# Three cross-attention tiles ahead of the loop instead of two

## The chip, the cores and the metric

The kernel runs on one NeuronCore of a Trainium2 chip. The metric is the device time of one launch in microseconds (us). Three runs of the kernel before took 3867.34, 3873.22 and 3873.66 us, so its median is 3873.22 us.

## The reference

One decoder layer is computed in float32 on x of shape 4 x 512 x 512 (2048 tokens, 512 channels), in three residual steps:

```python
x = x + attn(layernorm(x))           # gated delta rule, 16 heads, state 128 x 128 per head
x = x + xattn(layernorm(x), ctx)     # cross attention on 256 context rows, fake-quantised
x = x + ffn(layernorm(x))            # causal self attention with rope, then 2 of 8 experts
```

The cross attention of a token needs only that token's row after the first step: q = h Wq + bq, quantised per head; for each of 16 heads of width 32 the softmax over 256 keys, quantised to 255 levels; the weighted values; and a projection with Wp. The third step begins with a layer norm and an RMS norm of the result; keys, values and queries follow from that.

## The kernel before

All work is cut into 16 tiles of 128 tokens (NT = 16; a sequence is four tiles). There are three stages.

The first stage is the delta rule. It walks over 32 pairs of heads (NP = 32: four sequences by eight pairs). For pair m it runs `stage3(m)`, the recurrence over four chunks of 128 tokens, and beside it the output projection of pair m-1 (`output(m-1)`) and the preparation of later pairs. In the last two rounds the preparation has run out, so that little is left beside the recurrence. `output` of a sequence's last pair also scales the rows and writes them to DRAM (`x1d`), from which the cross attention reads its tiles (`xi`).

The second stage, the loop, is put together by `weave`. It holds four streams: `attention(i)` of tile i, `qkv(i)` 1.36 tiles ahead of it, the cross attention (`crossing(i)`, which carries `norms(i-1)` in its first steps) some tiles ahead, and what follows the attention (`rest_of`, `route`). Each stream is a chain of Python generators; `weave` gives every generator a start and a length in tiles and always takes the next step of the one that is furthest behind. The order written in this way is then arranged again by the compiler's scheduler, engine by engine[...].

The third stage runs the experts. It is not touched.

The pieces that the change concerns:

- `cross(i)` (lines 225 to 323) is one tile's cross attention. In order: layer norm (L131 to L137), transposes (L200), the query projection (L242), bias and quantisation (L244 to L217, on VectorE, ScalarE and GpSimd in turn), transposes (L200), four rounds of scores (L262), exponentials (L269), rounding (L274 on GpSimd, L278 on VectorE) and transposes (L287), the weighted values (L300), the output projection (L318), and bias and residual (L320, L321). It writes the result to DRAM (`x2d`, L322) and keeps it in SBUF as `x2`, a tile with two buffers.
- `xi` is loaded at the start of a cross attention (L232), or ahead by the one before it (L308), which before the change happens from tile 2 on.
- `norms(i)` (L1000 to L1018) reads `x2`, normalises twice and gives `hTs[i]`, which `qkv(i)` needs. `x3`, its tile in between, has one buffer and is stored to DRAM (`x3d`, L1006).
- In the last round of the first stage, `cross(0)` runs beside `stage3(31)` and `output(30)`, two steps of it for each step of the others. After that round `output(31)` and `cross(1)` run beside each other (L951). Then come the weights' first loads (`load_q`, `load_o`), `norms(0)` and the loop, whose cross attention begins with tile 2.
- `X` and `W` (L1325) are the lead and the spacing of the cross attention in the loop, in tiles.

`turns` takes its generators one after the other, each by its number of steps; `chain` runs them one behind the other. Loads and stores named `nc.sync` are issued by SyncE (SP in the profile), in order.

Of the kernel before, what the change touches and what calls it, by code (L numbers as in the profile page):

```python
# [40 lines left out]
NT = B * S // P  # L41
# [57 lines left out]
def decoder(ctx: ExitStack, tc: tile.TileContext, a: dict, out: bass.AP):  # L99
# [39 lines left out]
    def chain(*gs):  # L139
        for g in gs:  # L140
            yield from g
# [31 lines left out]
    def run(*gs):  # L173
        for g in gs:
            for _ in g:
                pass
# [50 lines left out]
    def cross(i):  # L227

        xi = xis.pop(i, None)
        if xi is None:  # L230
            xi = wx.tile([P, D], F32, name="xi", bufs=2)
            nc.sync.dma_start(xi, x1d[i])  # L232
            yield
            yield
        xn = wx.tile([P, D], F32, name="xn", bufs=1)
        yield from layernorm(xn.unsqueeze(1), xi.unsqueeze(1), wx)
        yield
        xT = transposed(xn, wx, "xT")
        yield
        pq = p_b.tile([P, D], F32, name="pb")  # L240
        for kd in range(KD):
            nc.tensor.matmul(pq, xT[:, kd, :], wq[:, kd, :], start=kd == 0, stop=kd == KD - 1)  # L242
        q = wx.tile([P, D], F32, name="xn", bufs=1)
        nc.vector.tensor_tensor(q, pq, bq, ALU.add)  # L244
        yield
        nc.scalar.mul(q, q, float(1.0 / np.sqrt(np.float32(HD2))))
        quantised(q, q, H2, HD2, wx)
        yield
        yield
        yield  # L250
        qT = transposed(q, wx, "x_qT", bufs=1)
        yield
        aT = wx.tile([P, KD, P], F32, name="xT")

        def scores(g0, r0, out):


            ps = [p_b.tile([P, 2, M], F32, name="pb") for _ in range(2)]
            for g in range(2):
                for r in range(2):  # L260
                    rs = slice((r0 + r) * HD2, (r0 + r + 1) * HD2)
                    nc.tensor.matmul(ps[r][:, g, :], qT[rs, g0 + g, :], x_kT[rs, g0 + g, :], start=True, stop=True)  # L262
            nm, ssum = (wx.tile([P, 4], F32, name=n) for n in ("nm", "ssum"))
            e = wx.tile([P, 4, M], F32, name="x_e")
            for r in range(2):
                nc.vector.tensor_reduce(nm[:, 2 * r : 2 * r + 2], ps[r], AX.X, ALU.max, negate=True)  # L266
                for g in range(2):
                    n = 2 * r + g
                    nc.scalar.activation(e[:, n, :], ps[r][:, g, :], AF.Exp, bias=nm[:, n : n + 1], accum_out=ssum[:, n : n + 1])  # L269
            yield  # L270


            ef = e.rearrange("p n m -> p (n m)")
            nc.gpsimd.tensor_scalar(ef, ef, 255.0, MAGIC, ALU.mult, ALU.add)  # L274
            nc.vector.tensor_scalar(ssum, ssum, 255.0, None, ALU.mult)
            nc.vector.reciprocal(ssum, ssum)
            yield
            nc.vector.scalar_tensor_tensor(e, e, MAGIC, along(ssum, M), ALU.subtract, ALU.mult)  # L278
            out.append(e)

        def turned(e, out):

            for r in range(2):
                tp = p_b.tile([P, 2, 2, P], F32, name="pb")
                for g in range(2):
                    for kt in range(2):
                        nc.tensor.transpose(tp[:, g, kt, :], e[:, 2 * r + g, kt * P : (kt + 1) * P], ident)  # L287
                eT = wx.tile([P, 2, 2, P], F32, name="x_eT", bufs=4)
                nc.scalar.copy(eT, tp)
                out.append(eT)  # L290
                yield

        def weighted(g0, eTs):

            pa = p_b.tile([P, 2, P], F32, name="pb")
            for g in range(2):
                for kt in range(2):
                    for r in range(4):
                        h = 4 * (g0 + g) + r
                        nc.tensor.matmul(pa[r * HD2 : (r + 1) * HD2, g, :], x_val[:, kt, h * HD2 : (h + 1) * HD2], eTs[r][:, g, kt, :], start=kt == 0, stop=kt == 1)  # L300
            nc.vector.tensor_copy(aT[:, g0 : g0 + 2, :], pa)
            yield

        es, eTs = [], []
        for u in range(5):
            if u == 3 and 1 < i < NT - 1:
                xis[i + 1] = wx.tile([P, D], F32, name="xi", bufs=2)
                nc.sync.dma_start(xis[i + 1], x1d[i + 1])  # L308
            if u < 4:
                yield from scores(u // 2 * 2, u % 2 * 2, es)  # L310
            if u > 0:
                yield from turned(es.pop(0), eTs)
            if u in (2, 4):
                yield from weighted(u - 2, eTs)
                eTs.clear()
        pw = p_b.tile([P, D], F32, name="pb")
        for kd in range(KD):
            nc.tensor.matmul(pw, aT[:, kd, :], wpj[:, kd, :], start=kd == 0, stop=kd == KD - 1)  # L318
        x2 = wx.tile([P, D], F32, name="x2", bufs=2)
        nc.vector.tensor_tensor(x2, pw, bp, ALU.add)  # L320
        nc.gpsimd.tensor_tensor(x2, x2, xi, ALU.add)  # L321
        nc.sync.dma_start(x2d[i], x2)  # L322
        x2s[i] = x2


    with ExitStack() as st:
# [593 lines left out]
        for m in range(NP):  # L920
            rest = []
            if m == NP - 2:
                first.close()
                x_keep = top.enter_context(tc.tile_pool(name="x_keep", bufs=1, side="right", reuse_waits="tile"))
                wq, wpj = (x_keep.tile([P, KD, D], F32, name=n) for n in ("wq", "wpj"))
                nc.sync.dma_start(wq, a["b_wq"].rearrange("(k p) c -> p k c", p=P))
                nc.sync.dma_start(wpj, a["b_wp"].rearrange("(k p) c -> p k c", p=P))
                bq, bp = rows(x_keep, "bq", "b_bq", D), rows(x_keep, "bp", "b_bp", D)
                x_kT, x_val = x_keep.tile([P, KD, M], F32, name="x_kT"), x_keep.tile([P, 2, D], F32, name="x_val")
                nc.sync.dma_start(x_kT, x_kT_d)  # L930
                nc.sync.dma_start(x_val, x_val_d)
            if m == NP - 1:
                second.close()
                wx = top.enter_context(tc.tile_pool(name="b_x", bufs=2, side="right", reuse_waits="tile"))
                rest.append((cross(0), 2))
            if m:
                rest.append((output(m - 1), 1))
            if m + 2 < NP:
                if (m + 2) % NHG == 0:
                    assert (m + 2) // NHG in seqs  # L940
                rest.append((stage1(m + 2), 2))
            if m + 1 < NP:
                rest.append((stage2_values(m + 1), 1))
                rest.append((stage2_inverse(m + 1), 2))
            if (m + 4) % NHG == 0 and (m + 4) // NHG < B:
                rest.append((prologue((m + 4) // NHG), 1))
            rest = turns(*rest)
            for _ in stage3(m):
                next(rest, None)
            run(rest)  # L950
        run(turns((output(NP - 1), 1), (cross(1), 2)))  # L951

# [7 lines left out]
    with ExitStack() as st:  # L962
# [37 lines left out]
        def norms(i):  # L1000


            x2 = x2s.pop(i)
            x3 = wq_.tile([P, D], F32, name="x3", bufs=1)
            yield from layernorm(x3.unsqueeze(1), x2.unsqueeze(1), small)
            nc.sync.dma_start(x3d[i], x3)  # L1006
            h = wq_.tile([P, D], F32, name="h3", bufs=1)
            ss = small.tile([P, 1], F32, name="rms_s")
            nc.scalar.activation(h, x3, AF.Square, accum_out=ss)
            yield  # L1010
            r = small.tile([P, 1], F32, name="rms_r")
            rsqrt(r, ss, small, add=1e-6, mul=1.0 / D)
            yield
            nc.vector.scalar_tensor_tensor(h, x3, r, ln1, ALU.mult, ALU.mult)
            yield
            hTs[i] = transposed(h, wq_, "hT", bufs=2)
            yield
# [276 lines left out]
        def crossing(i):  # L1294

            g = cross(i)
            return chain(turns((norms(i - 1), 1), (itertools.islice(g, 6), 1)), g)
# [24 lines left out]

        Q, X, W = 1.36, 3.1, 1.03  # L1325
        at_x = [(2 - X + (i - 2) * W, W, crossing(i), "cross") for i in range(2, NT)]
        at_x[-1] = (*at_x[-1][:2], last(chain(at_x[-1][2], norms(NT - 1))), "cross")
        at_q = [(i - Q, 1.0, qkv(i), "qkv") for i in range(NT)]
        at_q[-1] = (*at_q[-1][:2], last(at_q[-1][2]), "qkv")
# [2 lines left out]
        for i in range(NT - 1):  # L1332
# [3 lines left out]
            elif i == NT - 2:  # L1336
                g, kind = chain(g, route(12, 3)), "route"
            at_r.append((i + 1.06, 0.5, g, kind))
        run(norms(0))
        weave(at_a, at_q, at_x, at_r, [(NT - Q, 0.9, load_experts(), "load")])  # L1340
        w_gu, w_d = experts_w
        run(rest_of(NT - 1), route(NT - 1, 1))
# [182 lines left out]
```

## Time and profile before

| | before |
|---|---|
| median of three runs | 3873.22 us |
| the profiled execution, its own time | 3875.28 us |
| its span | 3873.5 us |
| PE busy | 3479.9 us (90%) |
| VectorE / ScalarE / GpSimd busy | 58% / 39% / 35% |
| last recurrence begins (first L704) | 2114.07 us |
| last matmul of cross(0) begins its group (L318) | 2164.06 us |
| last group of cross(1) (L318) | 2217.53 us |
| first projection of the loop (L1067) | 2221.49 us |
| last write of a cross attention result (L322) | 3425.4 us |
| first matmul of the last value product group (L1163), last start | 3565.8 us |

Times inside the execution count from the start of its span. A line such as L242 is a line of the kernel before. The profile of one matmul in float32 shows two instructions, so that eight L242 instructions are four matmuls. The timeline's columns are start, length, engine, line, operation, what is written and read, the number of merged instructions, and in brackets the idle time before them and what ended it.

### The profile page before, as it was taken

The page shows a single profiled execution, that of the slowest core. Times are in us where ns is not written, and L with a number is a line of the kernel's source. Part 1 is how long each engine was busy: PE and PEld are TensorE (multiplying, and loading weights), DVE is VectorE, ACT ScalarE, POOL GpSimd, SP SyncE. Part 2 cuts the span into 40 slices and gives each one's busy share as a digit, 9 for nine tenths or more (in the row PEclk, how much of TensorE's full clock was granted, in tenths as well). Part 3 has the DMA queues.
Part 4 walks back from the last instruction along what each step waited for, and adds up shares of the span by engine and source line. Part 5 has one row for each costly group of instructions (what it writes and reads, how often), then busy time and mean ns, then how long its engine had stood idle before and what let it go on. Part 6 is the DMA issues. An engine that isn't in the chain of part 4 may idle for free. (4 is left out here: it accounts for less than half of the span.)

```text
span 3873.5 us, 48929 instructions
## 1 busy us (share of the span) xinstructions
PE 3479.9 (90%) x16466; PEld 1984.5 (51%) x16466; DVE 2238.7 (58%) x5115; ACT 1523.7 (39%) x4190; POOL 1374.0 (35%) x1941
## 2 busy tenths in 40 slices
PE   5898989898989898989889879999999999898897
PEld 3455555555555555555545445555555555554443
DVE  5576657765766676657665546655665565554111
ACT  3334443334443434343433334444444444344121
POOL 1543554355335543554355222213212221211442
PEclk8899999998999999999999889999999999999898
DMA  5324332433234324333433245445544444456444
GB/s 163 109 71 126 104 103 78 130 104 114 78 106 129 104 77 120 105 102 100 120 88 111 72 154 161 139 147 158 163 132 140 145 139 141 137 174 206 82 82 92
DMA packets 391881, 465.56 MB, mean 120 GB/s; under 512 B 128451, under 2 KB 242115, under 8 KB 391440
## 3 DMA queue, kind: packets, MB, share of 16 engines
q1 hardware_dynamic: 380080, 438.03, 37.8%
q0 software_dynamic: 10112, 21.58, 3.1%
q8 instruction: 132, 2.16, 0.2%
q10 hardware_dynamic: 1440, 2.84, 0.2%
q14 instruction: 117, 0.96, 0.1%
HBM read 401.76 MB, written 64.81 MB: 120 GB/s over the span
## 5 line engine op out<-in xcount | busy, mean ns | idle before, releaser
L503 PE MATMUL pb<-xnT,w 128*128 128x512 f32 x2048 | 953.0, 604 | 0.0
L503 PEld LDWEIGHTS pb<-xnT,w 128*128 128x128 f32 x2048 | 381.0, 195 | 421.9 <-issue 417.8
L514 DVE SCALAR_TENSOR_TENSOR cv<-pb,pp,cv 128x511 f32<-128x511 f32 (+2 forms) x576 | 427.6, 742 | 153.0 <-ACT cv L511 144.0
L1067 PE MATMUL pb<-c_q,hT 128*128 128x512 f32 x768 | 360.7, 608 | 7.4 <-DMA c_q<-in_c_wq_dram 3.4
L644 POOL TENSOR_TENSOR iW<-iA,iT 32x31 f32<-32x31 f32 (+15 forms) x496 | 249.4, 503 | 212.3 <-DMA iA<-at_d 142.2
L825 PE MATMUL pb<-wot,og 128*128 128x512 f32 x512 | 265.9, 644 | 31.8 <-DVE og L796 26.5
L645 POOL TENSOR_TENSOR iT<-iT,iW 32x31 f32<-32x31 f32 (+15 forms) x496 | 275.2, 555 | 38.9
L511 ACT ACTIVATE cv<-pb,pp 128x512 f32<-128x512 f32 x192 | 148.2, 772 | 259.9 <-PE pb L503 259.4
L1173 PE MATMUL pw<-c_o,oT 128*128 128x512 f32 x512 | 241.8, 603 | 2.9 <-DVE oT L1165 2.9
L1067 PEld LDWEIGHTS pb<-c_q,hT 128*128 128x128 f32 x768 | 143.5, 195 | 165.4 <-issue 152.3
L1139 ACT ACTIVATE e<-pb,nm,rq 128x128 f32<-128x128 f32 (+3 forms) x256 | 157.0, 618 | 142.4 <-DVE nm L1137 108.8
L274 POOL TENSOR_SCALAR x_e<-x_e 128x1024 f32<-128x1024 f32 x64 | 68.7, 1074 | 329.4 <-ACT x_e L269 240.4
L644 DVE TENSOR_TENSOR iW<-iA,iT 32x31 f32<-32x31 f32 (+15 forms) x496 | 177.9, 359 | 12.4 <-DMA iA<-at_d 0.9
L645 DVE TENSOR_TENSOR iT<-iT,iW 32x31 f32<-32x31 f32 (+15 forms) x496 | 176.0, 355 | 11.9
L1163 PE MATMUL po<-eT,val 128*128 128x512 f32 x320 | 170.2, 625 | 6.9 <-ACT eT L1161 3.8
L558 POOL TENSOR_TENSOR rk<-ss,mhalf 128x8 f32<-128x8 f32 x32 | 53.1, 1658 | 317.9 <-DVE ss L557 317.8
L579 DVE SCALAR_TENSOR_TENSOR at<-pb,em 128x512 f32<-128x512 f32 x64 | 44.3, 692 | 208.5 <-ACT em L397 208.5
L1133 PE MATMUL pb<-kT,qT 128*128 128x256 f32 (+3 forms) x576 | 162.7, 409 | 0.8 <-ACT x_e L269 0.8
L269 ACT ACTIVATE x_e<-pb,nm 128x256 f32<-128x256 f32 x256 | 118.2, 477 | 101.9 <-DVE nm L266 101.9
L995 POOL TENSOR_TENSOR rope_s<-q,tab 128x128 f32<-128x128 f32 x64 | 35.4, 552 | 319.7 <-DVE q L1097 281.0
L825 PEld LDWEIGHTS pb<-wot,og 128*128 128x128 f32 x512 | 90.9, 197 | 110.3 <-issue 54.2
L397 ACT ACTIVATE em<-em,ee 128x128 f32<-128x128 f32 x256 | 78.6, 388 | 172.4 <-POOL ee L560 172.4
(324 smaller groups left out, 6742.1 us busy)
## 6 DMA issues: line engine op xcount, KB each, us to landing
c_o<-in_c_wo_dram SPq DMA_DIRECT2D x128, 512.0 KB, 4.1
c_q<-in_c_wq_dram SPq DMA_DIRECT2D x128, 512.0 KB, 4.7
w<-in_a_w_dram SPq DMA_DIRECT2D x124, 512.0 KB, 3.7
row<-g_d SPq DMA_DIRECT2D x64, 512.0 KB, 3.8
at_d<-at SPq DMA_DIRECT2D x64, 256.0 KB, 3.7
T<-t_d SPq DMA_DIRECT2D x32, 512.0 KB, 6.2
X<-x_d SPq DMA_DIRECT2D x32, 512.0 KB, 6.4
rrow<-r_d SPq DMA_DIRECT2D x32, 512.0 KB, 4.9
```

Of the source, the lines that this page charges most:

```text
L269: nc.scalar.activation(e[:, n, :], ps[r][:, g, :], AF.Exp, bias=nm[:, n : n + 1], accum_out=ssum[:, n : n + 1])
L503: nc.tensor.matmul(pj, wt[:, kd, p * P : (p + 1) * P], xnT[:, kd, :], start=kd == 0, stop=kd == KD - 1)
L511: nc.scalar.activation(ac, pj, AF.Identity, bias=cb[:, m, h : h + 1], scale=cw[:, m, h, 3:4])
L514: nc.vector.scalar_tensor_tensor(ac[:, j:], pj[:, : S - j], cw[:, m, h, 3 - j : 4 - j], ac[:, j:], ALU.mult, ALU.add)
L644: eng.tensor_tensor(u, A[:, i, i + 1 :].unsqueeze(2).to_broadcast([nb, n, w]), T[:, i, :w].unsqueeze(1).to_broadcast([nb, n, w]), ALU.mult)
L645: eng.tensor_tensor(T[:, i + 1 :, :w], T[:, i + 1 :, :w], u, ALU.add)
L825: nc.tensor.matmul(pw, og[p][:, c * P : (c + 1) * P], wot[:, p, :], start=p == 0, stop=p == HG - 1)
L1067: nc.tensor.matmul(pj, hT[:, kd, :], w[:, kd % 2, :], start=kd == 0, stop=kd == KD - 1)
L1133: nc.tensor.matmul(ps[:, m, k * P : (k + w) * P], qT[g][:, n + m, :], kT[:, g, j : j + w, :], start=True, stop=True)
L1139: nc.scalar.activation(e[n + m][:, :nk], ps[:, m, :nk], AF.Exp, bias=nm[:, n + m : n + m + 1], scale=rq, accum_out=es[:, n + m : n + m + 1])
L1163: nc.tensor.matmul(po, val[:, g, :], eT, start=k == 0, stop=k == c)
L1173: nc.tensor.matmul(pw, oT[:, h + m, :], w[:, m, :], start=g == 0 and h + m == 0, stop=g == 3 and h + m == 3)
```

## The change

The first-stage round for the last pair now takes the cross attention of tiles 0 and 1, one behind the other, four steps at a turn. Beside the last output projection runs that of tile 2. The loop's cross attention begins with tile 3, with a new lead and spacing. Since `x2` has two buffers and three tiles are done ahead of the loop, `norms(0)` reads its tile back from DRAM, into `x3`. `norms(0)` and `norms(1)` both run ahead of the loop. The next tile's `xi` is now loaded ahead from tile 0 on.

```diff
@@ in cross(i)
-            if u == 3 and 1 < i < NT - 1:
+            if u == 3 and i < NT - 1:
                 xis[i + 1] = wx.tile([P, D], F32, name="xi", bufs=2)
                 nc.sync.dma_start(xis[i + 1], x1d[i + 1])
@@ the last rounds of the delta rule
-                rest.append((cross(0), 2))
+                rest.append((chain(cross(0), cross(1)), 4))
...
-        run(turns((output(NP - 1), 1), (cross(1), 2)))
+        run(turns((output(NP - 1), 1), (cross(2), 2)))
@@ in norms(i)
             x3 = wq_.tile([P, D], F32, name="x3", bufs=1)
+            if i == 0:
+
+                nc.sync.dma_start(x3, x2d[i])
+                x2 = x3
             yield from layernorm(x3.unsqueeze(1), x2.unsqueeze(1), small)
@@ before the loop
-        Q, X, W = 1.36, 3.1, 1.03
-        at_x = [(2 - X + (i - 2) * W, W, crossing(i), "cross") for i in range(2, NT)]
+        Q, X, W = 1.36, 3.9, 1.08
+        at_x = [(3 - X + (i - 3) * W, W, crossing(i), "cross") for i in range(3, NT)]
...
-        run(norms(0))
+        run(norms(0), norms(1))
```

## The prediction

> **What bounds the kernel now.** I read the page's busy shares and its slices first, then busy time by stage, then the instructions in order of time at the seam between delta rule and loop. Slices:
>
> ```profile
> PE   5898989898989898989889879999999999898897
> PEclk8899999998999999999999889999999999999898
> ```
>
> The loop (slices 24 to 37) has PE at nine tenths or more: TensorE sets its pace. The seam is slices 22 and 23, with 8 and 7 tenths and a lower clock. Busy time by stage (length; PE, PE loads, VectorE, ScalarE, GpSimd busy; clock, DMA share, GB/s) splits it:
>
> ```profile
> 2114.00:2166.70 52.70, 44.85 (x334) 27.54 (x333) 31.94 (x65) 22.56 (x67) 14.80 (x13) 0.94 0.09 31
> 2166.70:2221.50 54.80, 39.73 (x182) 22.96 (x180) 27.76 (x56) 15.02 (x46) 13.82 (x16) 0.69 0.33 111
> 2221.50:2300.00 78.50, 61.23 (x247) 31.77 (x248) 31.89 (x66) 22.59 (x65) 17.66 (x26) 0.85 0.44 144
> 2300.00:2500.00 200.00, 193.55 (x849) 106.12 (x848) 128.15 (x327) 94.35 (x282) 42.69 (x60) 1.00 0.52 160
> ```
>
> The last recurrence with cross(0), output(31) with cross(1), the loop's start, its steady run. PE is idle 7.9 + 15.1 = 23 us in the first two: room, on paper, for a third cross attention. PE in order of time shows what fills the second:
>
> ```profile
> 2164.06 2.84 PE L318 MATMUL pb<-wpj,xT 128*128 128x512 f32 x6
> 2166.74 5.31 PE L825 MATMUL pb<-wot,og 128*128 128x512 f32 x12
> 2171.89 0.60 PE L200 MATMUL pb<-tab,xn 128*128 128x128 f32 x4
> 2173.17 3.70 PE L242 MATMUL pb<-wq,xT 128*128 128x512 f32 x8 [0.67 <-ACT xT L202]
> ...
> 2182.84 1.12 PE L200 MATMUL pb<-tab,xn 128*128 128x128 f32 x4 [4.26 <-POOL xn L217]
> 2184.63 2.11 PE L262 MATMUL pb<-x_kT,x_qT 32*128 32x256 f32 x16 [0.68 <-ACT x_qT L202]
> 2191.91 1.97 PE L287 MATMUL pb<-tab,x_e 128*128 128x128 f32 x8 [5.17 <-DVE x_e L278]
> ...
> 2217.53 2.84 PE L318 MATMUL pb<-wpj,xT 128*128 128x512 f32 x6
> 2220.21 0.60 PE L200 MATMUL pb<-tab,h 128*128 128x128 f32 x4
> 2221.49 7.13 PE L1067 MATMUL pb<-c_q,hT 128*128 128x512 f32 x16 [0.68 <-ACT hT L202]
> ```
>
> A cross attention with little beside it is a chain of latencies through four engines: cross(1) takes 2171.89 to 2220.2, 48.3 us; cross(0), between recurrence steps, 2124.16 to 2166.7, 42.5 us. And norms(0) had been done inside cross(1): its transposes stand right behind, so the loop begins 1.3 us after cross(1)'s last matmul.
>
> **What the skill says.** "TensorE: Matmul & The Clock Gate", Part 1 (the HAM clock gate): about 3.4 us of idleness halve TensorE's clock. The trace agrees: after the idle 4.26 and 5.17 us, eight L287 take 1.97 us, in cross(0) 1.09. The same page, Part 2, step 1: matmuls stay in program order, only weight loads are pulled ahead; so what PE's list puts behind a cross attention waits for it. "DMA: Bandwidth & Descriptors", Anatomy of one DMA and Queues, rings and completion order: a semaphore wait holds the issuing sequencer, and descriptors of SP's row start in ring order. The trace agrees:
>
> ```profile
> 2208.02 2.03 SPq L1043 DMA_DIRECT2D c_o<-in_c_wo_dram  x1
> 2222.47 0.34 SPq L322 DMA_DIRECT2D x2d<-x  x1
> 2222.86 1.57 SPq L1043 DMA_DIRECT2D c_o<-in_c_wo_dram  x2
> ...
> 2225.51 0.40 SPq L1006 DMA_DIRECT2D x3d<-x  x1
> ```
>
> SP stood 12 us at the store of cross(1)'s result; what followed waited for its end. The x3d store, behind 1.5 MB, landed at about 2231.5 (VectorE's L137 waited 2.4 us for it), 6 us against a median of 2.2.
>
> **The change part by part**, as the built order of the changed kernel has it.
>
> 1. *Third cross attention ahead of the loop.* PE's list has cross(0) earlier between the recurrence's steps, then cross(1)'s first transposes only behind cross(0)'s last L318, and its query projection among the last recurrence steps. From its second L200 to its L318 nothing stands beside it. Only then come output(31)'s L825, and cross(2) with them; its first L200 stands behind four of them. So three chains run one after another. Each costs 39.5 us at full clock (transposes, copy, L242 4.7; to the second L200 6.3; to the first scores 1.2; to the first L287 7.3, as in cross(1); 20.0 from there to the end, as in cross(0) from 2146.7 to 2166.7), and 48.3 as measured. From 2123 (the layer norm, as before, less 1 us), 42.5 + 47 + 48 plus 3 for output(31)'s first L825 gives 2263.5 for the last L318, against 2220.2: **+43 us**. Bounds: three at 39.5, +25; three at 48.3 with 10 us of mixing, +57. The L825, the x_in scaling (L843) and its GpSimd stores lie in those chains' gaps, as before. The early xi loads save the 1.1 us that L131 waited for xi at 2172.17.
>
> 2. *The reload.* In SP's list the load of x2d[0] into x3 stands behind the store of cross(2)'s result (which waits for L321), half of c_wv, three c_o and two padding stores. With T for the last L318's end: the store issues at T + 2.3, as before (2222.47 against 2220.2). Ahead of the load's end lie 4 x 512 KB + 2 x 256 KB + its own 256 KB = 2.75 MB. Before, 1.75 MB from 2222.9 to 2231.5 are 7 us at 0.25 MB/us plus some 2 us to land; so 11 + 2 us: it lands at T + 15.6. Behind it, by before's durations: three L131 (0.69), L132, L122, L123 (0.55), L131 of a later tile, L137, L1009 (0.85), L122, L123, L1014 (0.75): 6.6 us to h(0). norms(1), whose transposes PE's list puts ahead of the first projection, needs x3 free again: store issued at 4.1, landed 2.2 later, then L137, L1009, L122, L123, L1014 and L200 with their handovers, 3.7: the first projection at 10.5 behind the landing, T + 26, against T + 1.3: **+25 us**. VectorE's first L131, and behind it norms(1), norms(2) and the queue of qkv, wait on this load; PE has nothing else in its list. Bounds: +15 if the transfers run twice as fast and norms(1) costs 3 less; +30 if the store is later.
>
> 3. *One cross attention less in the loop.* By groups and shapes between 2300 and 3400 us, a cross attention's PE busy time is L200 16.4/13 + L242 47.8/13 + L262 66.1/12.75 + L287 61.0/12.5 + L300 30.8/12.5 + L318 43.4/12 = 21 us, in a stretch that is 96% busy: **-21 us**. Bounds: -8 (the loop's first tile waits more on chains than on PE: 17 of 78 us idle) and -35 (the waits of PE for cross attention's tiles there are some 28 us for 13 tiles; other spacing may avoid some).
>
> 4. *Lead, spacing, norms(1) ahead.* Another order of the same instructions. Norms become ready a little earlier against qkv at the end (13.14 against 13.32 tiles). norms(1)'s transposes leave the loop, 0.6 us. I take 0; its bounds are in part 3.
>
> Sum: 43 + 25 - 21 = +47. The profiled execution's own 3875.3 us (span 3873.5 and 1.8 around it) becomes 3922; it lies 2 us above the median shown, so the forecast is 3920.
>
> **Rivals.** *The reload is hidden* (SP comes to it sooner, or the transfers drain in half the time and norms run while cross(2) ends): part 2 falls to a few us, 3897. For it: 256 KB alone land in 2.5 us. Against: the store that waits for cross(2) stands ahead of it in the same queue. *The loop doesn't pay back* (the chain of attention or the pacing sets it): part 3 is -5, 3936. For it: PE is idle 41 us between 2300 and 3430 already. Against: the busy share. *Faster*: cross(1) and cross(2) overlap with what stands near them, since the seam has 23 us of idle PE and some 12 us lost to the halved clock. If the seam plus the reload grows by less than 21 us it decides for faster; filled ideally it grows by about 10, giving 3862. Against: PE's list is serial there, and each chain has at least 39.5 us. *The change doesn't do what it says*: the list shows one cross attention moved; no chance left for it.
>
> **How the numbers follow.** Forecast 0.60, hidden reload 0.14, no payback 0.16, faster 0.10 (0.03 of it within 0.2%). About 0.2%, 8 us, is what a measurement of this kernel can tell from no change. The likeliest case has its own range of 3900 to 3940; out to the rivals 3889 to 3944 leaves out the faster case and the worst tenth of bounds. Faster 0.07, same 0.03, slower 0.90.
>
> **What would show it.** Step 1: the last L318 ahead of the loop at about 2264, a stretch of some 30 us with only cross(1) on PE, at half clock. Step 2: a PE gap of about 25 us ahead of the first projection, VectorE waiting there on the load of x2d. Step 3: from the first projection to the last L1163, 21 us less than the 1344 before. It is wrong if the first projection comes before 2245, or the loop shrinks by over 40 us.

## The result and the profile after

The changed kernel takes 3943.2 us (median of five runs, 3933.2 to 3948.3) against 3872.0 (3865.5 to 3873.7) for the one before on the same chip: a ratio of 1.0182, 95% interval 1.0167 to 1.0198. The profiled spans are 3942.2 and 3873.5 us, 68.7 apart. Every ratio below is to runs of the kernel before on the same chip; stages are compared by the profiled executions.

The page's slices of the kernel after, to be laid beside those of before:

```profile
PE   5898899898988889889988669998999899999797
PEclk7899999899999999899999689999999899999898
```

The seam between delta rule and loop, which had 8 and 7 tenths in slices 22 and 23, now holds two slices of 6 tenths, and in the loop slice 27 has PE and slice 31 has the clock a tenth lower (slices counted from zero). Busy time by stage (length; PE, PE loads, VectorE, ScalarE, GpSimd busy; clock, DMA share, GB/s): the end of the recurrence with cross(0), cross(1), output(31) with cross(2), the gap, the loop.

```profile
2113.60:2169.60 56.00, 46.04 (x315) 27.62 (x316) 27.18 (x58) 20.59 (x63) 11.50 (x11) 0.85 0.09 33
2169.60:2221.00 51.40, 33.69 (x172) 20.63 (x171) 22.99 (x40) 15.56 (x47) 10.47 (x9) 0.63 0.03 11
2221.00:2273.00 52.00, 39.06 (x177) 22.21 (x175) 24.07 (x49) 14.02 (x43) 11.47 (x13) 0.67 0.31 97
2273.00:2296.60 23.60, 2.01 (x10) 1.63 (x9) 6.57 (x18) 1.93 (x5) 3.98 (x6) 0.56 0.59 194
2296.60:3634.60 1338.00, 1274.89 (x5443) 700.60 (x5442) 746.75 (x1950) 578.03 (x1587) 265.14 (x369) 0.97 0.49 152
```

The second row is new: 51.4 us with one cross attention, at a granted clock of 0.63. So is the fourth, 23.6 us with 2 us of PE work. From the loop's first projection to the last group of L1163 (L1167 after) before had:

```profile
2221.50:3565.80 1344.30, 1283.11 (x5597) 705.72 (x5598) 774.83 (x1995) 592.33 (x1632) 276.68 (x380) 0.98 0.50 154
```

The whole account, after less before, in us:

| | before | after | difference | forecast |
|---|---|---|---|---|
| start of the last recurrence | 2114.1 | 2113.6 | -0.5 | 0 |
| from there to the last L318 ahead of the loop | 106.1 | 159.4 | +53.3 | +43 |
| from its end to the first projection | 1.3 | 23.6 | +22.3 | +25 |
| loop | 1344.3 | 1338.0 | -6.3 | -21 |
| after the loop | 307.7 | 307.6 | -0.1 | 0 |

Both terms of the seam came out within their bounds (+25 to +57 and +15 to +30), the first 10 us over its forecast; the loop paid back less than a third of its share. PE in order of time across the seam of after:

```profile
2166.89 2.84 PE L318 MATMUL pb<-wpj,xT 128*128 128x512 f32 x6
2169.57 0.60 PE L200 MATMUL pb<-tab,xn 128*128 128x128 f32 x4
...
2175.95 0.39 PE L787 MATMUL po<-qg,state 128*128 128x128 f32 x2
2184.55 1.12 PE L200 MATMUL pb<-tab,xn 128*128 128x128 f32 x4 [8.21 <-POOL xn L217]
...
2218.18 2.84 PE L318 MATMUL pb<-wpj,xT 128*128 128x512 f32 x6
2220.86 3.60 PE L825 MATMUL pb<-wot,og 128*128 128x512 f32 x8
2224.29 0.60 PE L200 MATMUL pb<-tab,xn 128*128 128x128 f32 x4
...
2270.17 2.84 PE L318 MATMUL pb<-wpj,xT 128*128 128x512 f32 x6
2291.70 1.09 PE L200 MATMUL pb<-tab,h 128*128 128x128 f32 x4 [18.69 <-DVE h L1018]
2295.69 1.12 PE L200 MATMUL pb<-tab,h 128*128 128x128 f32 x4 [2.90 <-DVE h L1018]
2296.59 8.54 PE L1071 MATMUL pb<-c_q,hT 128*128 128x512 f32 x16
```

The recurrence ends at 2176, and from there to 2221 every instruction of PE is of cross(1): some 42 us up to the start of its last L318 group, where the prediction looked for 30. The three chains stand one behind the other, as PE's list has them. Then PE waits 18.7 us for h(0) and 2.9 for h(1). VectorE, and below it SP's own queue, name what h(0) waits for:

```profile
2285.98 1.29 DVE L131 BATCH_NORM_STATS2 ln_st<-x 128x6 f32<-128x512 f32 x2 [12.24 <-DMA x<-x2d]
```

```profile
2275.11 0.34 SPq L322 DMA_DIRECT2D x2d<-x  x1
2275.50 0.43 SPq L1038 DMA_DIRECT2D c_q<-in_c_wv_dram  x1
2275.97 1.53 SPq L1047 DMA_DIRECT2D c_o<-in_c_wo_dram  x3
2277.55 0.47 SPq L1059 DMA_DIRECT2D hd<-eT  x1
2278.06 0.48 SPq L1059 DMA_DIRECT2D acc<-eT  x1
2278.59 0.46 SPq L1007 DMA_DIRECT2D x<-x2d  x1
```

The reload (L1007) is issued 3.5 us behind the store of cross(2)'s result, and VectorE begins on it 7.4 us later. This looks like a full explanation of the gap. The experiments show that it isn't.

### The profile page after: what moved, and what is told of

It is laid out like the page before. It is cut to its first block, busy times and chain, and to the rows that moved or that the text cites. A ratio compares the mean times of both kernels' runs of the same rounds, so it can differ in the third digit from the quotient of the medians.

```text
span 3942.2 us, 48952 instructions
## 1 busy us (share of the span) xinstructions
PE 3506.0 (89%) x16466; PEld 1996.6 (51%) x16466; DVE 2231.6 (57%) x5115; ACT 1524.2 (39%) x4190; POOL 1369.4 (35%) x1941
## 5 line engine op out<-in xcount | busy, mean ns | idle before, releaser
L825 PE MATMUL pb<-wot,og 128*128 128x512 f32 x512 | 265.4, 643 | 32.0 <-DVE og L796 26.5
L1177 PE MATMUL pw<-c_o,oT 128*128 128x512 f32 x512 | 241.4, 602 | 16.5 <-DVE oT L1169 16.3
L1167 PE MATMUL po<-eT,val 128*128 128x512 f32 x320 | 173.3, 638 | 12.7 <-ACT eT L1165 9.5
L1177 PEld LDWEIGHTS pw<-c_o,oT 128*128 128x128 f32 x512 | 91.8, 190 | 113.4 <-issue 86.2
L825 PEld LDWEIGHTS pb<-wot,og 128*128 128x128 f32 x512 | 90.3, 196 | 110.8 <-issue 55.0
```

Source lines behind the costliest of these rows:

```text
L825: nc.tensor.matmul(pw, og[p][:, c * P : (c + 1) * P], wot[:, p, :], start=p == 0, stop=p == HG - 1)
L1167: nc.tensor.matmul(po, val[:, g, :], eT, start=k == 0, stop=k == c)
L1177: nc.tensor.matmul(pw, oT[:, h + m, :], w[:, m, :], start=g == 0 and h + m == 0, stop=g == 3 and h + m == 3)
```

## Experiments on the seam

**Keep x2, no reload.** A third x2 buffer makes the reload unnecessary; cross attention's turned q shares xT's buffers, to make room.

```diff
-        qT = transposed(q, wx, "x_qT", bufs=1)
+        qT = transposed(q, wx, "xT")
...
-        x2 = wx.tile([P, D], F32, name="x2", bufs=2)
+        x2 = wx.tile([P, D], F32, name="x2", bufs=3)
...
-            if i == 0:
-                nc.sync.dma_start(x3, x2d[i])
-                x2 = x3
```

> The changed kernel with three buffers for x2, so that norms(0) reads its tile from SBUF and nothing is read back; the room comes from letting the transposed q share the two buffers of the transposed x. Theory R (the reload behind the store of cross(2) costs what lies between): the first projection follows the last L318 by about 1.5 us instead of 23.7, 22 us less, 3921. Rival (the start waits for the weights' first pieces, whose loads stand in the same queue): the gap shrinks by at most 5, 3938 or more.

Ratio 1.0154 (1.0137 to 1.0171). The seam is 5.7 us shorter, not 22, and the gap 6.8, so neither of the two expectations was met. PE around the end of cross(2) in this kernel:

```profile
2268.18 2.84 PE L318 MATMUL pb<-wpj,xT 128*128 128x512 f32 x6
2271.81 0.66 PE L200 MATMUL pb<-tab,h 128*128 128x128 f32 x4 [0.78 <-DVE x L320]
2286.95 1.11 PE L200 MATMUL pb<-tab,h 128*128 128x128 f32 x4 [14.49 <-DVE rsq L122]
```

h(0) is turned 0.8 us after the end of the last L318, where after took 18.7. But then PE stands 14.5 us at the transposes of h(1), which its list puts ahead of the first projection. VectorE and SP's queue in the same kernel:

```profile
2283.99 0.55 DVE L137 TENSOR_SCALAR x<-x,ln_mv,ln_rs 128x512 f32<-128x512 f32 x1 [9.95 <-DMA x3d<-x]
```

```profile
2273.12 0.34 SPq L322 DMA_DIRECT2D x2d<-x  x1
...
2276.69 0.41 SPq L1006 DMA_DIRECT2D x3d<-x  x1
```

norms(1) writes x3, which has one buffer; it must wait for norms(0)'s store of x3d, and that store stands in the same place in SP's queue, behind cross(2)'s store and the weights, as the reload did. One wait took the other's place.

**norms(1) in the loop**, with the reload and without it.

```diff
+        at_x[0] = (*at_x[0][:2], chain(norms(1), at_x[0][2]), "cross")
...
-        run(norms(0), norms(1))
+        run(norms(0))
```

> After, with the second tile's norms moved from ahead of the loop into the loop, ahead of the first crossing; the reload of x2[0] stays. Theory A (reload and norms(1) are two delays in series; the reload's chain ends with norms(0)'s transposes, norms(1)'s come only 4 us later): the first projection comes some 20 us behind the last matmul of cross(2) instead of 23.7, time near 3939. Theory B (the reload alone makes the gap, as the prediction has it): the same, 20 to 22. This run is the other half of the pair with the next one.

> After, with x2 kept in a third buffer, so no reload, and the second tile's norms moved into the loop. Theory A (each of the two delays alone holds the first projection up): gap 1 to 3 us instead of 23.7, so 20 less in the seam and about 3921. Theory B (the reload alone is the cause, and what was left in the run that only kept x2 has another reason, in SP's queue or in the weights): the gap stays at about 16 us, as there, and the time near 3936.

The four kernels make a square (gap from the end of the last L318 to the first projection, us; ratio to before):

| | norms(1) ahead of the loop | norms(1) in the loop |
|---|---|---|
| reload | 23.6; 1.0182 (after) | 20.5; 1.0162 (1.0143 to 1.0181) |
| x2 kept | 16.8; 1.0154 | 2.1; 1.0132 (1.0115 to 1.0149) |

Either repair alone saves 3 to 7 us of the gap; both together save 21.5. Their loops are alike (1338.0, 1337.6, 1340.2, 1337.8). PE of the kernel with both:

```profile
2265.86 2.84 PE L318 MATMUL pb<-wpj,xT 128*128 128x512 f32 x6
2269.48 0.66 PE L200 MATMUL pb<-tab,h 128*128 128x128 f32 x4 [0.79 <-DVE x L320]
2270.81 7.13 PE L1067 MATMUL pb<-c_q,hT 128*128 128x512 f32 x16 [0.68 <-ACT hT L202]
```

So the gap has two causes, each enough for most of it: the reload, and norms(1) ahead of the first projection with its single x3. Theory A held.

**Two chains side by side.** cross(0) beside the last recurrence at before's pace, cross(1) and cross(2) together beside output(31); the third works in buffers of the delta rule that are free by then. x2 is kept, as above, and norms(1) stays ahead of the loop. Not shown in the cut: one `yield` less in `output`, and xi of tiles 2 and 3 is no longer loaded ahead.

```diff
-                rest.append((chain(cross(0), cross(1)), 4))
+                rest.append((cross(0), 2))
...
-        run(turns((output(NP - 1), 1), (cross(2), 2)))
+        run(turns((output(NP - 1), 1), (cross(1), 2), (cross(2, True), 2)))
```

> Tile 0 beside the last recurrence as in the kernel before (two steps a turn), tiles 1 and 2 side by side, step for step, beside the last output projection; the second of them keeps its tiles in buffers that the recurrence has left; x2 has three buffers, nothing is read back; the loop begins with tile 3 as in the changed kernel. Theory S (a cross attention at the seam is a chain of latencies, and costs its 48 us only because the chains stand one after another): from the last recurrence's first matmul to the first projection 107 to 117 us instead of 183, and the time 3866 to 3882 with the loop as it is, so within 10 us of the kernel before. Rival (the third one costs its own 21 us of PE or more wherever it stands): 128 us or more, 3888 or more.

Ratio 1.0084 (1.0062 to 1.0107). From the last recurrence's start to the last L318 it takes 121.8 us, against 159.4 in after and 106.1 in before with one cross attention fewer. By the number that was expected, up to the first projection, it is 141.3 us: not the 107 to 117 of theory S, because a gap of 19.5 us follows, so the 3908.4 us of the whole kernel lie on the rival's side. PE of this kernel shows two query projections 6.5 us apart between the L825:

```profile
2175.46 3.70 PE L242 MATMUL pb<-wq,xT 128*128 128x512 f32 x8 [0.68 <-ACT xT L202]
2179.00 1.88 PE L825 MATMUL pb<-wot,og 128*128 128x512 f32 x4
2180.71 0.60 PE L200 MATMUL pb<-tab,qg 128*128 128x128 f32 x4
2181.99 3.70 PE L242 MATMUL pb<-wq,at 128*128 128x512 f32 x8 [0.67 <-ACT at L202]
```

Up to the last L318 the third cross attention costs about 16 us here instead of 53, less than its own 21 us of PE work: what made it dear was that the chains stood one behind the other, not the work. The gap behind it is that of norms(1) again; PE and VectorE:

```profile
2257.02 1.12 PE L200 MATMUL pb<-tab,h 128*128 128x128 f32 x4 [18.15 <-DVE h L1013]
```

```profile
2254.06 0.55 DVE L137 TENSOR_SCALAR x<-x,ln_mv,ln_rs 128x512 f32<-128x512 f32 x1 [12.60 <-DMA x3d<-x]
```

## Experiments on the loop

The loop's first long stall in after is 12 us of PE, and VectorE's record names a suspect, the constants' copy of a later route (L1281), which stands behind the first route's scatters and waits for them:

```profile
2738.42 2.07 PE L1177 MATMUL pw<-c_o,oT 128*128 128x512 f32 x2 [12.08 <-DVE oT L1169]
```

```profile
2736.93 0.24 DVE L1281 COPY r_entry<-tab 128x4 f32<-128x4 f32 x2 [15.95 <-DMA lists<-r_entry,r_place]
```

**More route buffers**, and **the slots of before** for the loop's cross attentions, each alone in after:

```diff
-            place = small.tile([P, n, 2], mybir.dt.int32, name="r_place", bufs=2)
-            entry = small.tile([P, n, 2, 2], F32, name="r_entry", bufs=2)
+            place = small.tile([P, n, 2], mybir.dt.int32, name="r_place", bufs=5)
+            entry = small.tile([P, n, 2, 2], F32, name="r_entry", bufs=5)
```

> The changed kernel with five buffers instead of two for the two small tiles of the routing (r_entry, r_place), so that a later tile's copy need not wait until the scatters of an earlier one have landed. Theory A (the loop lost its payback to VectorE's 16 us wait at such a copy, of which PE lost 12.1 us, and to the halved clock behind it): the wait is gone, the loop from the first projection to the last value product shrinks from 1338 us by 12 to 18, to about 1323, the time from 3943 to about 3927. Theory B (lead and spacing of the cross attention set the loop): the loop stays within 4 us of 1338, 3939 to 3947.

```diff
-        Q, X, W = 1.36, 3.9, 1.08
+        Q, X, W = 1.36, 3.07, 1.03
```

> The changed kernel with the loop's cross attention started and spaced as before (lead 3.07, spacing 1.03: tile 3 at -0.07, the end at 13.32 tiles, as in the kernel before). Theory A (a copy hoisted in front of the scatters costs the payback): no systematic gain, the loop moves only as far as the copy comes to stand elsewhere, 1333 to 1343, 3938 to 3948. Theory B (lead and spacing): the loop shrinks by 10 to 15, 3928 to 3933.

With more buffers the copy no longer waits, and the longest of PE's waits at L1177 is 2.0 us. The loop gets 7.1 us shorter in the profiled execution, which was the slowest of four (3942.9 us; median 3932.1). By the ratio (1.0138, 1.0118 to 1.0159, against 1.0182) the kernel gains 0.44%, some 17 us, so the wait is worth 7 to 17 us: theory B (within 4 us) is out, and theory A (12 to 18) not settled. With the slots of before (the same times as in before for every tile from the fourth, i = 3, on) the loop gets 36.5 us shorter: 1301.5, ratio 1.0097 (1.0079 to 1.0114), although the copies still wait 10 us there. That is far more than either expectation allowed. Busy time of the loops with more buffers and with the slots of before, to be laid beside the last of the rows by stage shown for after:

```profile
2302.50:3633.40 1330.90, 1275.81 (x5442) 701.24 (x5442) 744.48 (x1944) 577.76 (x1587) 265.08 (x369) 0.97 0.50 153
2302.30:3603.80 1301.50, 1253.11 (x5442) 689.19 (x5442) 752.12 (x1950) 578.52 (x1587) 267.08 (x369) 0.99 0.50 156
```

With the slots of before, the same number of PE instructions, within one, is 21.8 us shorter in busy time than in after, and PE's idle time is 14.7 us shorter (48.4 against 63.1). The busy time goes with the clock (0.99 against 0.97): the trace's clock records show half speed for 37 us of this loop and for 85 of after's. Work done in those 48 us would have taken 24 at full speed, an estimate that about covers the 21.8.

**One cross attention less, and nothing else moved.** This is before, with the third tile's cross attention (i = 2) left out of the loop, so that this part of the result is missing; empty steps keep its slot.

```diff
     def cross(i):
+        if i == 2:
+            x2 = wx.tile([P, D], F32, name="x2", bufs=2)
+            nc.sync.dma_start(x2, x1d[i])
+            nc.sync.dma_start(x2d[i], x2)
+            x2s[i] = x2
...
+            return
```

> Before, with the cross attention of the third tile left out of the loop (its x2 is a copy of x1, so this part of the result is not computed) and its slot and all other slots, and everything ahead of the loop, as in before. It measures what one cross attention less in the loop's beginning is worth by itself. By the prediction's third step: loop 21 us shorter (1323), time 3852. If what the loop gains is more than the work (less halved clock at its beginning), as the run with the slots of before suggests: loop 1300 to 1308, time near 3833. If the loop doesn't give it back: 1336 or more.

Ratio 0.9902 (0.9880 to 0.9923), 3834.3 us. Its loop:

```profile
2213.90:3523.70 1309.80, 1264.54 (x5446) 694.91 (x5446) 754.66 (x1961) 578.22 (x1589) 269.35 (x373) 0.98 0.51 158
```

1309.8 against 1344.3: one cross attention less is worth 34.5 us at the slots of before, 18.6 of it PE's busy time and 15.9 idle time. The ratio says 38 us (30 to 46). That is more than the forecast 21, and about its outer bound of 35; the time is that of the second expectation. So after's -6.3 is -34.5 and, for lead and spacing, +28.2.

**Lead or spacing?** After with only the spacing of before, and after with the spacing of before and a tenth more of lead than it:

```diff
-        Q, X, W = 1.36, 3.9, 1.08
+        Q, X, W = 1.36, 3.9, 1.03
```

> After with its lead of 3.9 and the spacing of before, 1.03: every cross attention of the loop stands 0.83 of a tile earlier than in before, at the end of the loop too. If the lead is what costs the loop (the early cross attentions stand in the queues where attention and routes need PE and VectorE): loop near after's 1338, halved clock near 85, 3940 to 3948. If it is the wider spacing (cross attention falls due against the same tile's attention in a drifting place): loop near 1302, halved clock near 45, 3910.

```diff
-        Q, X, W = 1.36, 3.9, 1.08
+        Q, X, W = 1.36, 3.17, 1.03
```

> After with lead 3.17 and spacing 1.03: a tenth of a tile earlier than the run with 3.07. If pacing acts smoothly, the loop stays within 6 us of that run's 1301.5 (time 3908 to 3920). If it acts by which instruction happens to stand ahead of which, so that small shifts are as good as large ones, the loop moves by 15 us or more.

Their loops, the lead alone first:

```profile
2292.40:3610.90 1318.50, 1260.20 (x5443) 694.11 (x5442) 744.75 (x1950) 577.25 (x1587) 264.85 (x369) 0.98 0.50 154
2291.20:3597.80 1306.60, 1258.10 (x5444) 692.65 (x5442) 747.00 (x1950) 576.86 (x1587) 263.47 (x369) 0.98 0.51 156
```

| lead, spacing | loop | PE busy | PE idle | halved clock | ratio |
|---|---|---|---|---|---|
| 3.07, 1.03 | 1301.5 | 1253.1 | 48.4 | 37 | 1.0097 |
| 3.17, 1.03 | 1306.6 | 1258.1 | 48.5 | 53 | 1.0099 (1.0076 to 1.0121) |
| 3.9, 1.03 | 1318.5 | 1260.2 | 58.3 | 61 | 1.0123 (1.0093 to 1.0153) |
| 3.9, 1.08 (after) | 1338.0 | 1274.9 | 63.1 | 85 | 1.0182 |

(Halved clock is the time at half speed in the trace's clock records between the loop's first projection and its last L1167.) Neither of the two expectations for the lead alone held: of the 36.5 us, by these loops of one execution each, about 17 are the lead's and about 19.5 the spacing's. The spacing's share is clear of noise in the ratios too (1.0123 and 1.0182, intervals apart, some 23 us); the lead's isn't (1.0097 and 1.0123, intervals that overlap, some 10 us). A tenth of a tile of lead moves the loop by 5 us and the ratio not at all: no jump, as expected if pacing acts smoothly. Two kernels with the same slots and nearly the same loop, 1301.5 and 1309.8, stand 8 us apart, so differences below that mean little. Which instruction's place in the order costs the most wasn't settled: most of the added idle time lies in two stretches. PE is idle 15.1 us in the loop's first 200 us and 15.1 between 400 and 600, against 9.4 and 6.6 with the slots of before. The stall at L1177 is in the second; taking away its wait gave back 7 us of the loop in the execution that was traced.

**After's slots in before**, the same times for every tile from the fourth on (the expectation counts from zero; the lead is counted from i = 2, where before's loop begins):

```diff
-        Q, X, W = 1.36, 3.1, 1.03
+        Q, X, W = 1.36, 3.98, 1.08
```

> Before, with after's slots for the loop's cross attentions (lead 3.98 counted from the second tile, spacing 1.08: the same times for every tile from the third on). Theory A (the slots cost the loop by themselves, some 30 to 40 us): the time near 3905 (3890 to 3920), halved-clock time in the loop up from 65 to 85 or more. Theory B (the slots only cost where one cross attention is missing from the loop's beginning): within 8 us of before.

Ratio 1.0110 (1.0093 to 1.0127): near theory A's number, but for another reason. The loop as cut here is only 6.0 us longer (1350.3), with 93 us at half speed against 65; the seam is 41.6 longer. The lead of 3.98 puts the first crossing ahead of the first projection, and with it norms(1) and part of cross(2). PE of this kernel:

```profile
2215.65 0.60 PE L200 MATMUL pb<-tab,h 128*128 128x128 f32 x4
2229.63 1.12 PE L200 MATMUL pb<-tab,h 128*128 128x128 f32 x4 [13.39 <-DVE rsq L122]
...
2258.72 2.44 PE L1067 MATMUL pb<-c_q,hT 128*128 128x512 f32 x4
```

It shows the wait of norms(1) once more, 13.4 us, in a kernel that has no reload. As a measure of the slots it is mixed and decides nothing.

## The repairs together

cross(1) and cross(2) side by side, x2 kept, norms(1) in the loop (as a stream of its own), slots of before, five route buffers. The last two pieces of its edit against after:

```diff
-        Q, X, W = 1.36, 3.9, 1.08
+        Q, X, W = 1.36, 3.07, 1.03
...
-        run(norms(0), norms(1))
+        at_x.insert(0, (-0.9, 0.4, norms(1), "norms"))
+        run(norms(0))
```

> All repairs together: cross(0) beside the last recurrence, cross(1) and cross(2) side by side beside the last output projection, x2 kept in a third buffer, norms(1) in the loop, lead and spacing of before (3.07 and 1.03 counted from the third), five buffers for the route's lists. If the seam's costs and the loop's add up: seam 122 to 126, loop 1295 to 1301, about 3850 (3840 to 3862), faster than before. If the gains do not add (the loop takes back what the seam gives, as norms(1) and the early projections meet cross attention again): 3870 or more.

3864.8 us, ratio 0.9965 (0.9948 to 0.9982): faster than before, by a third of a per cent, but 15 us slower than the 3850 expected, between the two expectations. The seam is 126.9 us (gap 2.7), 0.9 above what was added up; the loop is 1315.2, where its parts promised 1295 to 1301:

```profile
2244.60:3559.80 1315.20, 1267.70 (x5446) 695.21 (x5446) 756.04 (x1957) 578.53 (x1589) 268.87 (x373) 0.98 0.51 159
```

PE's idle time is down (47.5 us, as with the slots of before alone); its busy time is 14.6 us longer than there, at a lower clock (61 us at half speed against 37), for four instructions more. Part of this may be the execution: the profiled one was the slowest of nine, which took 3845.0 to 3869.2 us. Why the clock is lower was not tried.

## Why the prediction was right on the sign and short on the size

The measured 3943.2 us lie above the likeliest case's range (3900 to 3940) and 0.8 us inside the wider one (to 3944). Single executions took 3933 to 3948, so on which side of that bound the median fell was luck.

- **Step 1, the third cross attention in series, +43:** right in mechanism, +52.8 from 2220.2 to 2273.0. cross(0) ended at 2169.6 instead of 2165.5; cross(1), almost alone and at a clock of 0.63, took 51.4 instead of 47: the idle time ahead of its second L200 was 8.21 us where before had 4.26. cross(2) took 48.7 for 48, behind 3.3 us of L825 for 3. The side-by-side run shows that the series was the cause. One reading was wrong, though it stands in no sum: the 1.1 us that L131 waited at 2172.17 belong to cross(2), for cross(1)'s transposes had begun at 2171.89.
- **Step 2, the reload, +25:** the size held (+22.3), the cause only in part. VectorE began on the reloaded tile 13.0 us behind the last L318's end (forecast: landed at 15.6), and the first projection came 10.6 us behind that (forecast 10.5). But the step laid nearly the whole delay on the reload, and its rival took the delay down to a few us if the reload were hidden. Without the reload 16.8 us of the gap remain. The step saw the single x3 and its store, and 2.2 us for that store's landing was right behind the reload: issued at 2289.23, free for VectorE at 2291.65, 2.4 us later. Without the reload the same store stands behind cross(2)'s result and the weights: issued at 2276.69, and VectorE got x3 at 2283.99, 7.3 us later.
- **Step 3, one cross attention less, -21:** mis-sized. At unchanged slots it measured -34.5: 18.6 us of busy time, near the 21 forecast, and 15.9 us of idle time that went with it. The step had named those waits, but only as a bound.
- **Step 4, lead and spacing, 0:** this is the step that failed, and the largest error. "Another order of the same instructions" costs 28.2 us net of step 3, 36.5 against the same kernel with the slots of before. The same instructions ran at a lower clock and with more idle time.
- **Rivals:** "the loop doesn't pay back" (-5, 3936) came nearest, and for the reason it named, the pacing; yet its meaning that the loop could not pay back is refuted by the kernel with one cross attention less. "The reload is hidden" falls with the gap of 23.6 us. "Faster" falls for this order. Cross attentions that overlap at the seam, its condition, had to be written, and even then (1.0084) the kernel became faster only with all the repairs together.

In the sum the errors were +10, -3 and +15 on terms of +43, +25 and -21: 22 us, from 47 to 69. The last of them is itself what is left of two that partly cancel: -13.5 in step 3 and +28.2 in step 4.

## What to carry to other kernels

Before pricing a delay by the one transfer that ends last, look in the engine's list for the next thing that needs the same queue: here two waits ended nearly together, and the repairs gave 6.8 and 3.1 us alone but 21.5 together. A change of lead or spacing in a hand-paced loop is an edit of its own, to be given a bound of both signs of its own: with the same instructions it was worth 36 us of 1338, as much as the work that was moved (34.5). And when a chain of latencies is moved to a place with little else to do, put it beside another chain, not behind it: 16 us instead of 53.

## What was not expected of the hardware

A copy of four columns (0.24 us for two of them) held VectorE for 15.95 us because it waited for scatters of two values a row to land; taking away this wait gave 7 us of loop in the traced execution and some 17 by the ratio. And PE's busy time for the same loop, 5442 to 5444 instructions, lay between 1253.1 and 1275.8 us in the five kernels shown; the time at half speed in the clock records went along, from 37 to 85 us. In after, the 12.1 us wait that ends at 2738.4 lies in a spell at half speed from 2729.7 to 2743.4, so that the two matmul instructions behind it took 2.07 us together, where one takes 0.60 on average. Idle time explains this only in part: five route buffers took 8.0 us of idle time away (55.1 against 63.1) and none of the busy time (1275.8 against 1274.9).
